# Gate logits and q.bk with the weights stationary on four column groups of TensorE

## The chip, the cores and the metric

The kernel runs on one core of one Trainium2 chip. The metric is device time in microseconds (us) of one execution, the median over several runs. Engines are called PE (TensorE), VectorE (DVE), ScalarE (ACT), POOL (GpSimd) and SyncE (SP, which only issues DMAs here).

## What is computed

One layer of a perceiver in float32, on x of 8 x 64 rows of 512 and a context of 8 x 1601 rows: cross attention, an attention with 16 heads and sigmoid scores, and a mixture of 8 experts with one expert for each row. Cut to what the change touches:

```python
# cross attention
qp = layernorm(x) @ Wq + bq
kp = ctx @ Wk + bk
logits = (qp @ kp.T) / sqrt(512)      # = (qp @ Wk.T @ ctx.T + qp . bk) / sqrt(512)
x = x + softmax(logits) @ (ctx @ Wv + bv)
# ... attention with 16 heads ...
# experts, on layernorm(x)
logits = xn @ gate_w.T                # 8 logits for each row
top_v, sel = max(logits), argmax(logits)
rw = sigmoid(top_v)                   # xs = xn * rw goes to expert sel
```

## The kernel before

The 512 rows of x are four tiles of 128 rows (two batches each, called a pair p, or tile i). All products are float32; a row of 512 is four chunks of 128 on the partitions (dc or ec).

**Order of the work.** PE's order is written out by hand over the whole kernel (`manual_schedule`); the other engines are ordered by a planner, save in a few stretches, and each runs its instructions in its order. PSUM has eight banks of one shape (`bank`); SBUF tiles come from pools: 12 slabs of 128 x 2048 (context groups, weights, xnT, qpT), 22 rows, 5 blocks (`blk`). A load into a slab is issued by SyncE when the slab's last reader is done.

**Start.** `normal`, `turn_x` and `project_q` make qpT, the projected queries with features on the partitions, first for tile 0, then for tiles 1 to 3. `keyed(p)` multiplies them with Wk (p_qk), `biased(p)` with bk: four products of 128 x 128 stationary qpT with one moving column give q.bk of the 128 rows in a PSUM column, and ScalarE copies it to `qb[:, p]`. `spread` (POOL) and `fill_queries` (PE transposes rt, ScalarE copies) lay the keyed queries out as R.

**Pair by pair.** For p in 0 to 3: the context (cx) is transposed by VectorE in blocks (`blocks`, `turn_group`, L233 and L240); `scores` multiplies them with R in four quarters q of 32 products each, into four banks sc; `softmax` uses qb in VectorE's nb and bias (L375, L377) and ScalarE's exponentials; `chance` (pp) turns them, `attend` (ac) sums the context in four groups g. In p = 0, `keyed` and `biased` of pairs 1 to 3 and `tables` come between softmax and the first `chance`. `tables` makes gwc, the gate weights less their mean, 128 x 4 x 8.

**Gates.** The second attention and the gates of tile i run inside the passes of later pairs (i = p - 2) for tiles 0 and 1 and in the hand-written tail for tiles 2 and 3. `face` transposes x into x3T; `gated` calls `gate`: four products of stationary x3T chunks with 8 moving columns of gwc (L682, pl), then on VectorE the row moments, the maximum (top), a one-hot (oh); ScalarE takes the sigmoid rw. `routed` finds the row's slot with products pr of oh and running sums, and POOL scatters the scaled rows to DRAM; `fetch` (SyncE) reads them back by expert, `flip` (t_xe, xeT), `up_first` and `up_last` (gu, four experts on four column groups of 32), `over` (ht) and `down` (y) apply the experts.

Of the kernel before, what the change touches and what calls it, by code (L numbers as in the profile page):

```python
# [36 lines left out]
def perceiver_kernel(ctx: ExitStack, tc: tile.TileContext, out: bass.AP, t: dict):  # L37
# [16 lines left out]
    def row(name):  # L54
        return rowp.tile([P, D], F32, tag="row", name=name)
# [4 lines left out]
    def bank(name):  # L60
        return banks.tile([P, D], F32, tag="bank", name=name)

    def bank4(name):
        return banks.tile([P, DC, P], F32, tag="bank", name=name)
# [37 lines left out]
    def load_b(name, n, c=None):  # L102
        if c is None:
            c = const.tile([P, n], F32, tag=name, name=f"c_{name}")
        tc.keep_in_program_order(
            nc.gpsimd.dma_start(out=c, in_=t[name].partition_broadcast(P))
        )
        return c
# [203 lines left out]
        qks[p] = row(f"qk{p}")  # L312
        nc.scalar.copy(qks[p], ps)

    def biased(p):

        cols = slice(p * P, (p + 1) * P)
        ps = bank(f"qb{p}")
        for ec in range(DC):
            nc.tensor.matmul(  # L320
                ps[:, 0:1], lhsT=qpT[:, ec, cols],
                rhs=bk[:, ec : ec + 1], start=(ec == 0), stop=(ec == DC - 1),
            )
        nc.scalar.copy(qb[:, p : p + 1], ps[:, 0:1])  # L324

    def spread(p):

# [17 lines left out]
    def fill_queries(p, R, q4s, half):  # L345
        for b0 in range(8 * half, 8 * half + 8, 4):
            tp = bank4(f"rt_{p}_{b0}")
            for j in range(4):
                nc.tensor.transpose(
                    tp[:, j, :], q4s[b0 // 4][:, j, :, :].rearrange("p a d -> p (a d)"), ident  # L350
                )
            nc.scalar.copy(R[:, b0 : b0 + 4, :], tp)
# [56 lines left out]
    def attend(p, g, pt, ac):  # L409
        cx = cxs.pop((p, g))  # L410
        nch, m = extent(g)
        for j in range(nch):
            for b2 in range(2):
                r = b2 * S
                rhs = cx[b2][:, j, :] if g < 3 else cx[b2][:m, :]
                nc.tensor.matmul(  # L416
                    ac[r : r + S, :], lhsT=pt[:m, j, r : r + S], rhs=rhs,
                    start=(g == 0 and j == 0), stop=(g == 3),
                )
# [225 lines left out]
    before = const.tile([P, P], F32, tag="before", name="before")  # L645
    iot = const.tile([P, E], I32, tag="iot", name="iot")
    rev = const.tile([P, E], F32, tag="rev", name="rev")
    gwc = const.tile([P, DC, E], F32, tag="gwc", name="gwc")

    def tables():  # L650
        nc.gpsimd.memset(ones, 1.0)
        nc.gpsimd.memset(before, 1.0)
        nc.gpsimd.affine_select(
            before, before, pattern=[[1, P]], base=0, channel_multiplier=-1,
            compare_op=ALU.is_gt, fill=0.0,
        )
        nc.gpsimd.iota(iot, pattern=[[-1, E]], base=E, channel_multiplier=0)
        nc.gpsimd.tensor_copy(rev, iot)
        ps = bank("gs")
        nc.tensor.matmul(  # L660
            ps[:, : DC * E], lhsT=ones, rhs=gwT.rearrange("p c e -> p (c e)"),
            start=True, stop=True,
        )
        mean = tiny(E, "gmean", "gmean")
        nc.vector.tensor_reduce(
            mean, ps[:, : DC * E].rearrange("p (c e) -> p e c", e=E), AX.X, ALU.add
        )
        nc.vector.tensor_scalar(mean, mean, -1.0 / D, None, ALU.mult)
        nc.vector.tensor_tensor(
            gwc, gwT, mean.unsqueeze(1).to_broadcast([P, DC, E]), ALU.add  # L670
        )

    runs = []

    def gate(i):


        x3T = tile_of[i]["x3T"]
        ps = bank(f"pl{i}")
        pl = ps[:, :E]  # L680
        for dc in range(DC):
            nc.tensor.matmul(  # L682
                pl, lhsT=x3T[:, dc, :], rhs=gwc[:, dc, :],
                start=(dc == 0), stop=(dc == DC - 1),
            )
        mean, rs = spread_v(xs[i], f"c{i}")

        top = tiny(1, "top", f"top{i}")
        nc.vector.tensor_reduce(top, pl, AX.X, ALU.max)
        nc.scalar.activation(rw[:, i : i + 1], top, AF.Sigmoid, scale=rs)  # L690
        wt = tiny(E, "wt", f"wt{i}")
        nc.vector.scalar_tensor_tensor(wt, pl, top, rev, ALU.is_equal, ALU.mult)
        first = tiny(1, "first", f"first{i}")
        nc.vector.tensor_reduce(first, wt, AX.X, ALU.max)
        nc.vector.tensor_scalar(oh[:, i, :], wt, first, None, ALU.is_equal)

        begin = tiny(1, "begin", f"begin{i}")
        skip = (NT - 2) * PART * (E - 1) if i == NT - 1 else 0
        nc.vector.tensor_scalar(begin, first, -PART, E * PART + skip, ALU.mult, ALU.add)
        return mean, rs, begin  # L700
# [114 lines left out]
    def face(i):  # L815
        x3T = row4(f"x3T{i}")
        nc.scalar.copy(x3T, transposed(xs[i], f"x3_{i}"))
        tile_of[i]["x3T"] = x3T

    def gated(i):  # L820
        d = tile_of[i]
        d["spread"] = gate(i)
# [23 lines left out]
    def do(*steps):  # L846
        for f, i in steps:
            f(i)

    with tc.manual_schedule(engines={mybir.EngineType.Activation}):  # L850
        keyed(0)
        for i in range(1, NT):
            turn_x(i, later[i - 1])
        biased(0)
    q4s = spread(0)
    project_q(1, NT - 1, [bank(f"qp1_{ec}") for ec in range(DC)])
    R = queries(0)
    fill_queries(0, R, q4s, 0)
    fill_queries(0, R, q4s, 1)
    bv = load_b("xbv", D, row("c_xbv"))  # L860
    lnw = load_late("lnw", [P, DC])
    lnb = load_late("lnb", [P, DC])
# [9 lines left out]
    for p in range(NT):  # L872
        i = p - 2
        if 0 < p < NT - 1:
            q4s = spread(p + 1)
        sc = [bank(f"sc_{p}_{a}") for a in range(4)]
        for q in range(4):
            if p == 0 and q == 0:
                nTs = [first[1, 0], first[1, 1]]
            elif p == 0 and q == 1:  # L880
                nTs = [first[2, 0], blocks(0, 2, 1)]
            else:
                nTs = quarter(p, q + 1) if q < 3 else None
            if i >= 0 and q == 3:
                scores(p, q, R, sc, Ts, range(3))
                do((back, i))
                scores(p, q, R, sc, Ts, (3,))
            else:
                scores(p, q, R, sc, Ts)
            Ts = nTs  # L890
            if i >= 0 and q < 3:
                do(((split, align, sums)[q], i))
        L, r = softmax(p, sc)
        pts = []

        def chance():
            pts.append(chances(p, len(pts), L))

        if p == 0:
            for k in range(1, NT):  # L900
                keyed(k)
                biased(k)
                if k == 1:
                    q4s = spread(1)
            tables()
        else:
            do((at_turn, p - 1))
            if i >= 0:
                do((output, i))
        if p + 1 < NT:  # L910
            R = queries(p + 1)
            if p == 0:
                chance()
                fill_queries(1, R, q4s, 0)
            elif p == 1:
                fill_queries(2, R, q4s, 0)
                do((at_out, 0))
                chance()
            else:
                do((at_out, p - 1))  # L920
                fill_queries(p + 1, R, q4s, 0)
                chance()
            fill_queries(p + 1, R, q4s, 1)
        else:
            at_out(p - 1, chance)
        if 0 < p < NT - 1:
            load_pair(p + 1)
        if p == 1:
            blank_rows()
        ac = bank(f"ac_{p}")  # L930
        if i >= 0:
            do((face, i))
        for g in range(4):
            if g < 3:
                chance()
            if p > 0 and g == 3:
                do((turn, p - 1))
            attend(p, g, pts[g], ac)
            if p > 0 and g == 0:
                do((norm, p - 1))  # L940
            if i >= 0 and g == 0:
                do((gated, i))
            if i >= 0 and g == 1:
                do((routed, i))
        tile_of[p]["acs"] = divided(p, ac, r)
        if 0 < p < NT - 1:
            do((unit_q, p - 1))
            Ts = quarter(p + 1, 0)
            do((unit_k, p - 1), (gates, p - 1), (values, p - 1))
        elif p == 0:  # L950
            Ts = quarter(1, 0)
# [82 lines left out]
    do((unit_q, 3), (over, 0), (sums, 2))  # L1034
    unit_k(3, lambda: back(2))
    do((flip, 1), (output, 2))
    do((split, 3), (gates, 3), (face, 2), (values, 3), (gated, 2), (align, 3), (up_first, 1))
    do((routed, 2))
    fetch(1)
    do((sums, 3), (up_last, 1), (back, 3), (down, 0), (output, 3), (over, 1), (flip, 2))  # L1040
    do((flip, 3), (face, 3), (up_first, 2), (gated, 3), (up_last, 2), (routed, 3))
    fetch(2)

    ps = bank("pc")
# [128 lines left out]
```

## Time and profile before

| what | us |
| --- | --- |
| median of 3 runs | 298.19 |
| lowest and highest | 298.16, 298.40 |
| the profiled execution | 297.94 |
| its span, from the first to the last instruction | 296.2 |

One execution is profiled, on the chip. "Busy" of PE is from the start of a product to its modelled end, and products overlap, so the mean of a row is a latency and the distance between starts is what a product costs. PEld is the load of stationary weights. The busy row of forty slices gives tenths of 7.4 us each. In a group, the numbers after the first bar are busy us and mean ns, those after the second the idle time of the engine just before, and what ended most of it. A timeline row has start, length, engine, line, operation and tiles (out<-in), the shape, the count, and in brackets the idle time before it with its releaser. A SyncE wait row has the total, the number and the longest.

### The profile page before, as it was taken

The numbers are of one execution on the slowest core, as the hardware profiler recorded it, in microseconds if no ns is written. First come the engines' busy times: TensorE is split into PE (matmuls) and PEld (weight loads), VectorE is DVE, ScalarE is ACT, GpSimd is POOL, SyncE is SP. The second block draws the span as 40 slices with busy tenths as digits, with TensorE's granted clock in tenths as the row PEclk, the third lists the DMA queues.
The fourth block names the chain that finished last, engine by engine and source line by source line (L and its number), as shares of the span: only waits on it lengthen the run. The fifth ranks groups of instructions, "written<-read, shape, count | busy, mean of one in ns | idle before, by whom it ended". The sixth has DMA issues, their size and how long they took to land. (4 is left out here: it accounts for less than half of the span.)

```text
span 296.2 us, 6460 instructions
## 1 busy us (share of the span) xinstructions
PE 284.2 (96%) x2652; PEld 145.4 (49%) x2652; DVE 159.0 (54%) x412; ACT 92.1 (31%) x202; POOL 64.0 (22%) x109
## 2 busy tenths in 40 slices
PE   6999899999999999999999999999999999999992
PEld 4866655653654334655634465544455456353320
DVE  2464477226654377856668795463272457364140
ACT  2222304340019121236814143651515534120110
POOL 4065200600071101600211310032050032412302
PEclk9999999999999999999999999999999999999998
DMA  6999970179986895000199300959991200523501
GB/s 186 350 408 397 340 318 1 19 284 358 424 292 226 289 385 214 6 3 0 24 387 379 135 2 10 358 198 318 383 375 67 73 0 2 173 74 113 175 3 42
DMA packets 20288, 57.71 MB, mean 195 GB/s; under 512 B 2274, under 2 KB 10514, under 8 KB 16544
## 3 DMA queue, kind: packets, MB, share of 16 engines
q1 hardware_dynamic: 17568, 50.37, 47.5%
q0 software_dynamic: 2400, 6.89, 6.2%
q8 instruction: 23, 0.38, 0.5%
q14 instruction: 9, 0.07, 0.1%
q10 hardware_dynamic: 288, 0.00, 0.1%
HBM read 50.94 MB, written 6.84 MB: 195 GB/s over the span
## 5 line engine op out<-in xcount | busy, mean ns | idle before, releaser
L233 DVE STREAM_TRANSPOSE T<-cx 128x512 f32<-128x512 f32 x96 | 61.8, 680 | 25.2 <-DMA cx<-in_ctx_dram 18.6
L360 PE MATMUL sc<-T,R 32*64 32x416 f32 (+2 forms) x1024 | 49.5, 501 | 1.8 <-DVE T L233 1.2
L416 PE MATMUL ac<-cx,pt 128*64 128x512 f32 x192 | 43.8, 598 | 0.0
L360 PEld LDWEIGHTS sc<-T,R 32*64 32x64 f32 x1024 | 26.6, 131 | 19.3 <-issue 7.1
L416 PEld LDWEIGHTS ac<-cx,pt 128*64 128x64 f32 x192 | 12.7, 136 | 22.4 <-issue 21.6
L981 PE MATMUL gu<-wgu,xeT 128*32 128x512 f32 x192 | 23.0, 597 | 0.0
L492 POOL TENSOR_TENSOR gm_k<-qn_k,c_gk 128x512 f32<-128x512 f32 x4 | 5.1, 1271 | 61.0 <-DVE qn_k L487 61.0
L284 PE MATMUL qp<-xnT,w_xWq 128*128 128x128 f32 (+1 forms) x64 | 16.3, 426 | 0.5 <-ACT xnT L275 0.5
L455 POOL TENSOR_TENSOR x<-x,c_bo 128x512 f32<-128x512 f32 x4 | 5.1, 1270 | 54.3 <-DVE xh L454 54.3
L332 POOL COPY q<-qk 128x512 f32<-128x512 f32 x16 | 9.0, 612 | 34.5 <-ACT qb L324 21.4
L185 PE MATMUL p_qk<-w_xWkT,qpT 128*128 128x512 f32 x32 | 14.9, 605 | 0.0
L185 PE MATMUL p_q<-w_aWq,xhT 128*128 128x512 f32 x32 | 14.8, 605 | 0.0
L185 PE MATMUL p_k<-w_aWk,xhT 128*128 128x512 f32 x32 | 14.7, 595 | 0.0
L185 PE MATMUL p_po<-w_xWv,acT 128*128 128x512 f32 x32 | 14.7, 595 | 0.0
L406 ACT COPY pt<-pp 128x512 f32<-128x512 f32 (+1 forms) x16 | 8.3, 516 | 20.4 <-PE pp L404 20.2
L185 PE MATMUL p_o<-w_aWo,cT 128*128 128x512 f32 x32 | 14.5, 596 | 0.0
L371 DVE TENSOR_REDUCE mx<-sc 128x1 f32<-128x416 f32 (+2 forms) x16 | 8.1, 567 | 11.9 <-PE sc L360 11.9
L185 PE MATMUL p_v<-w_aWv,xvT 128*128 128x512 f32 x32 | 14.4, 592 | 0.0
L284 PEld LDWEIGHTS qp<-xnT,w_xWq 128*128 128x128 f32 x64 | 11.6, 232 | 5.0 <-ACT xnT L275 0.9
L1016 PE MATMUL y<-wd,hT 128*32 128x512 f32 x96 | 11.5, 596 | 0.6 <-DVE hT L1008 0.6
L981 PEld LDWEIGHTS gu<-wgu,xeT 128*32 128x32 f32 x192 | 6.0, 109 | 8.9 <-issue 8.2
L185 PEld LDWEIGHTS p_q<-w_aWq,xhT 128*128 128x128 f32 x32 | 5.7, 189 | 9.0 <-issue 5.9
(190 smaller groups left out, 392.1 us busy)
## 6 DMA issues: line engine op xcount, KB each, us to landing
cx<-in_ctx_dram SPq DMA_DIRECT2D x24, 1024.0 KB, 10.0
wgu<-in_wgT_dram SPq DMA_DIRECT2D x8, 512.0 KB, 9.5
wgu<-in_wuT_dram SPq DMA_DIRECT2D x8, 512.0 KB, 10.3
wd<-in_wdT_dram SPq DMA_DIRECT2D x8, 512.0 KB, 8.9
rd<-blank POOLq DMA_DIRECT2D x6, 258.0 KB, 4.8
in<-rd SPq DMA_DIRECT2D x6, 258.0 KB, 4.6
xd<-blank POOLq DMA_DIRECT2D x6, 256.0 KB, 4.6
in<-xd SPq DMA_DIRECT2D x6, 256.0 KB, 7.2
```

The costliest lines, as they stand in the source:

```text
L185: nc.tensor.matmul(ps, lhsT=srcT[:, dc, :], rhs=w[:, dc, :], start=(dc == 0), stop=(dc == DC - 1),)
L233: nc.vector.transpose(T[:, :, 128 * g : 128 * g + 128].rearrange("p b (c k) -> p b c k", k=32), cxs[p, g][b2][:, :, 128 * q : 128 * q + 12 ...
L284: nc.tensor.matmul(ps[ec][:, : n * P], lhsT=wq[:, dc, ec * P : (ec + 1) * P], rhs=xnT[:, dc, cols], start=(dc == 0), stop=(dc == DC - 1),)
L332: nc.gpsimd.tensor_copy(q4, qk[:, 32 * b0 : 32 * b0 + 128].rearrange("p (b d) -> p b d", d=32).unsqueeze(2).to_broadcast([P, 4, 4, 32]),)
L360: nc.tensor.matmul(sc[a][r : r + S, : WIDTH[a]], lhsT=R[32 * a : 32 * a + 32, b, r : r + S], rhs=Ts[b2][32 * a : 32 * a + 32, j, : WIDTH[a ...
L371: nc.vector.tensor_reduce(mx[:, a : a + 1], sc[a][:, : WIDTH[a]], AX.X, ALU.max)
L406: nc.scalar.copy(pt[:m, :nch, :], tp[:m, :nch, :])
L416: nc.tensor.matmul(ac[r : r + S, :], lhsT=pt[:m, j, r : r + S], rhs=rhs, start=(g == 0 and j == 0), stop=(g == 3),)
L455: nc.gpsimd.tensor_tensor(xs[i], xs[i], bo, ALU.add)
L492: nc.gpsimd.tensor_tensor(heads(gm), heads(qn), gb.unsqueeze(1).to_broadcast([P, H, HD]), ALU.mult)
L981: nc.tensor.matmul(ps[c, :], lhsT=xTs[k][:, dc, c], rhs=ffw[e][0][:, dc, :], start=(dc == 0), stop=(dc == DC - 1),)
L1016: nc.tensor.matmul(y[c, :], lhsT=hT[:, ic, c], rhs=ffw[e][1][:, ic, :], start=(ic == 0), stop=(ic == IC - 1),)
```

## The change

`biased` now serves all pairs at once. The stationary operand is a chunk of bk, one column repeated 32 times; the moving operand is qpT of one pair, 128 columns. Pair p writes PSUM partitions 32p to 32p + 31, so the four pairs use the four groups of 32 columns of the array. ScalarE copies the result (qbT), `unturned` transposes it on PE after quarter 0 of the first scores, and VectorE copies every 32nd column to qb. The four calls of `biased(p)` go.

The gate is cut in two. `gate_parts` (new step `logits`) holds the gate weights stationary, padded to 32 columns (POOL fills gwc with zeros first), with x3T moving; chunk dc writes partitions 32dc to 32dc + 31, so each group holds a partial sum. ScalarE copies it to `shares`. `gate` then adds the four parts and turns them by one product of stationary shares with the 0/1 table `pick` (made from the identity by VectorE). Between the two halves stand: for tiles 0 and 1 the transposes of the next `chance`, for tile 2 the products of `align`, for tile 3 the transposes of `flip(3)`, which before came ahead of `face(3)`.

```diff
-    def biased(p):
-        cols = slice(p * P, (p + 1) * P)
-        ps = bank(f"qb{p}")
+    def biased():
+        ps = bank("qb")
         for ec in range(DC):
-            nc.tensor.matmul(
-                ps[:, 0:1], lhsT=qpT[:, ec, cols],
-                rhs=bk[:, ec : ec + 1], start=(ec == 0), stop=(ec == DC - 1),
-            )
-        nc.scalar.copy(qb[:, p : p + 1], ps[:, 0:1])
+            for p in range(NT):
+                nc.tensor.matmul(
+                    ps[32 * p : 32 * p + 32, :P],
+                    lhsT=bk[:, ec : ec + 1].to_broadcast([P, 32]),
+                    rhs=qpT[:, ec, p * P : (p + 1) * P],
+                    start=(ec == 0), stop=(ec == DC - 1),
+                )
+        qbT = rowp.tile([P, P], F32, tag="row", name="qbT")
+        nc.scalar.copy(qbT, ps[:, :P])
+        return qbT
+
+    def unturned(qbT):
+        tp = bank4("t_qb")
+        nc.tensor.transpose(tp[:, 0, :], qbT, ident)
+        nc.vector.tensor_copy(qb, tp[:, 0, ::32])
...
-    gwc = const.tile([P, DC, E], F32, tag="gwc", name="gwc")
+    gwc = const.tile([P, DC, 32], F32, tag="gwc", name="gwc")
+    pick = const.tile([P, E], F32, tag="pick", name="pick")
...
+        nc.gpsimd.memset(gwc, 0.0)
         nc.vector.tensor_tensor(
-            gwc, gwT, mean.unsqueeze(1).to_broadcast([P, DC, E]), ALU.add
+            gwc[:, :, :E], gwT, mean.unsqueeze(1).to_broadcast([P, DC, E]), ALU.add
+        )
+        nc.vector.tensor_reduce(
+            pick, ident.rearrange("p (c k) -> p k c", k=32)[:, :E, :], AX.X, ALU.add
         )
...
+    def gate_parts(i):
+        x3T = tile_of[i]["x3T"]
+        ps = bank(f"pg{i}")
+        for dc in range(DC):
+            nc.tensor.matmul(
+                ps[32 * dc : 32 * dc + 32, :P], lhsT=gwc[:, dc, :], rhs=x3T[:, dc, :],
+                start=True, stop=True,
+            )
+        shares = rowp.tile([P, P], F32, tag="row", name=f"shares{i}")
+        nc.scalar.copy(shares, ps[:, :P])
+        return shares
+
     def gate(i):
-        x3T = tile_of[i]["x3T"]
         ps = bank(f"pl{i}")
         pl = ps[:, :E]
-        for dc in range(DC):
-            nc.tensor.matmul(
-                pl, lhsT=x3T[:, dc, :], rhs=gwc[:, dc, :],
-                start=(dc == 0), stop=(dc == DC - 1),
-            )
+        nc.tensor.matmul(pl, lhsT=tile_of[i]["shares"], rhs=pick, start=True, stop=True)
...
         keyed(0)
         for i in range(1, NT):
             turn_x(i, later[i - 1])
-        biased(0)
...
     fill_queries(0, R, q4s, 1)
+    qbT = biased()
...
+            if p == 0 and q == 0:
+                unturned(qbT)
...
                 keyed(k)
-                biased(k)
...
+            if i >= 0 and g == 1:
+                do((gated, i))
             attend(p, g, pts[g], ac)
...
             if i >= 0 and g == 0:
-                do((gated, i))
+                do((logits, i))
...
-    do((split, 3), (gates, 3), (face, 2), (values, 3), (gated, 2), (align, 3), (up_first, 1))
+    do((split, 3), (gates, 3), (face, 2), (values, 3), (logits, 2), (align, 3), (gated, 2), (up_first, 1))
...
-    do((flip, 3), (face, 3), (up_first, 2), (gated, 3), (up_last, 2), (routed, 3))
+    do((face, 3), (up_first, 2), (logits, 3), (flip, 3), (gated, 3), (up_last, 2), (routed, 3))
```

More of the change, by code (lines that the diff above doesn't have):

```diff
@@ L818, in face, with logits @@
         tile_of[i]["x3T"] = x3T
+    def logits(i):
+        tile_of[i]["shares"] = gate_parts(i)
     def gated(i):
```

## Prediction, made before the result

> **What bounds the kernel now.** I read the busy table first, then the forty slices, then the groups, the timelines of the stages that the diff touches, and SyncE's own waits. The page:
>
> ```profile
> span 296.2 us, 6460 instructions
> PE 284.2 (96%) x2652; PEld 145.4 (49%) x2652; DVE 159.0 (54%) x412; ACT 92.1 (31%) x202; POOL 64.0 (22%) x109
> ...
> PE   6999899999999999999999999999999999999992
> ```
>
> TensorE (PE) is busy in nearly the whole span, from slice 7 to the last but one without a gap. Its instruction order is written by hand. What leaves PE in that stretch should leave the span; what leaves PE earlier, where slices 5 and 6 show 8 and 9, has to be looked at one wait at a time. The chain of waits names only the last scatter, so I don't lean on it. The operations that the diff replaces, in the groups kept apart by shape:
>
> ```profile
> L981 PE MATMUL gu<-wgu,xeT 128*32 128x512 f32 x192 | 23.0, 597 | 0.0
> ...
> L682 PE MATMUL pl<-gwc,x3T 128*128 128x8 f32 x32 | 4.1, 255 | 0.0
> ...
> L320 PE MATMUL qb<-c_xbk,qpT 128*128 128x1 f32 x32 | 3.8, 240 | 0.0
> ```
>
> Four gates of four products are 16 products but 32 records, so each f32 product is two passes. The column "128*32" of gu is rows times columns of the array in use. The means are latencies; spacing is what costs, and the timeline has it:
>
> ```profile
> 45.41 3.70 PE L185 MATMUL p_qk<-w_xWkT,qpT 128*128 128x512 f32 x8
> ...
> 48.95 0.95 PE L320 MATMUL qb<-c_xbk,qpT 128*128 128x1 f32 x8
> ...
> 49.76 3.68 PE L185 MATMUL p_qk<-w_xWkT,qpT 128*128 128x512 f32 x8
> ...
> 53.28 0.95 PE L320 MATMUL qb<-c_xbk,qpT 128*128 128x1 f32 x8
> ...
> 54.09 3.68 PE L185 MATMUL p_qk<-w_xWkT,qpT 128*128 128x512 f32 x8
> ```
>
> From one p_qk to the next 4.35 and 4.33 us pass; eight passes of p_qk take 3.43 (p_k to p_v: 110.03 to 113.47 = 3.44). So one `biased(k)` costs 0.90 us of PE for one useful column: eight weight loads 0.11 apart.
>
> **What the Trainium skill says.** "TensorE: Matmul & The Clock Gate", LDWEIGHTS: a load costs by its columns, about P/1.2 ns, 107 ns for 128. The trace agrees: 0.90 / 8 = 0.11 us. "TensorEngine Tiling (Array Packing)", Performance Considerations: with few moving columns, swap stationary and streaming and use column tiles; and Key Properties: changing the tiling mode drains the array. The trace shows both: gu on four column groups runs 16 passes of 512 columns in 1.92 us, the time of four, and between modes the starts are 0.08 to 0.15 us further apart (pl to the al products, ht to gu). No row of before has four column groups with only 128 moving columns.
>
> **The change part by part.** Times are from the profiled execution: 297.94 us with a span of 296.2, 0.25 under the median 298.19.
>
> 1. `biased(0)` goes from ahead of the second q projection. Worth 0: that projection starts at 18.86 because ScalarE's xnT copies end at 18.80; PE then idles for those 0.9 us. If that cover were gone it would gain 0.9.
>
> 2. `biased()` for all pairs comes after the first R transposes: 16 products, 32 passes, four groups at a time, so 8 rounds. A round is one pass of 128 columns, 0.11 us (transposes start 0.109 apart): 0.88, and a drain 0.1, about 1.0 us. It lies ahead of the scores, which wait:
>
> ```profile
> 31.12 0.91 PE L360 MATMUL sc<-T,R 32*64 32x416 f32 x2
> ...
> 33.26 8.64 PE L360 MATMUL sc<-T,R 32*64 32x416 f32 x192 [1.23 <-DVE T L233]
> ...
> 36.38 1.90 DVE L233 STREAM_TRANSPOSE T<-cx 128x512 f32<-128x512 f32 x3 [2.59 <-PE sc L360]
> ...
> 42.15 0.26 DVE L240 STREAM_TRANSPOSE T<-tail 96x128 f32<-96x128 f32 x1
> ...
> 42.47 3.02 PE L360 MATMUL sc<-T,R 32*64 32x416 f32 x62 [0.57 <-DVE T L240]
> ```
>
> Scores start at 31.12 but stand until 33.26 for VectorE's blocks, which wait for the context's DMA. 2.14 us of cover for 1.0: worth 0. ScalarE's copy qbT (0.27, as the 128x128 hT copy takes) comes after the R copies, ahead of 16 us in which ScalarE waits.
>
> 3. `unturned`: after quarter 0 of the scores PE does one transpose (0.11, two mode changes: about 0.35 in all), and VectorE copies four columns, between two block transposes. VectorE is the bound here: from 36.38 it makes three pairs of blocks without a pause and PE waits 0.57 for the last. PE's 0.35 fits into the 0.57. VectorE's first block transpose runs 36.38 to 37.0 while PE turns qbT (ready near 36.7), so no new wait; the copy inserts 0.05 (as small operations between transposes do at 153.2) to 0.2: **+0.1**. Queued behind it are the blocks of quarters 2 and 3, which PE waits for.
>
> 4. `biased(1..3)` go from between the p_qk: 3 x 0.90 = **-2.70**, on PE where it has no gap; three copies of one column (0.16) leave ScalarE. What must keep up: ScalarE's exponentials end at 52.6 in either case, then it copies qk1; POOL's q4 copies run 53.3 to 55.6, and their transposes come on PE near 56.4. ScalarE's six copies after that end near 59.5, before attend needs more than the first. The loads of pair 1 wait on SyncE for slabs:
>
> ```profile
> SPq L212 <- PE p_qk L185: 27.4, 1, 27.4
> ...
> SPq L212 <- PE qb L320: 0.4, 1, 0.4
> ```
>
> The slab of WkT comes free with the last p_qk (issue at 57.80), that of qpT with the last qb; both come 1.7 to 2.5 us earlier, on a DMA idle since 44 us. So the pair's blocks move along, and all later loads hang on PE releases.
>
> 5. Gates 0 and 1, inside attend:
>
> ```profile
> 146.41 1.06 PE L682 MATMUL pl<-gwc,x3T 128*128 128x8 f32 x8
> ...
> 147.33 0.64 PE L404 MATMUL pp<-ident,L 128*128 128x128 f32 x4
> ...
> 147.89 3.65 PE L416 MATMUL ac<-cx,pt 128*64 128x512 f32 x16
> ```
>
> Before: 1.48 us from pl to ac. After: pg 2 rounds 0.22, drain 0.1, pp 0.44, pl as one product 0.22, drain 0.12: 1.10, if shares is there. Its chain: pg's last pass is issued at +0.11 and lands +0.28 later, ScalarE follows 0.09 on, copies 0.27, PE 0.05 on: +0.80, against PE at +0.76. Nearly a tie. Bounds: 0 gained if ScalarE is 0.4 late, 0.38 at best; I take **-0.25 each**. The sigmoid's table load (1.28) now stands after the pt copy; the row weight is then ready near 149.9, VectorE needs it by 151.9 (its wait for pr). Covered.
>
> 6. Gate 2: from the end of p_v to gu 1.91 us before. After: 0.1 + 0.22 + 0.1 + 1.02 (al with its drain) + 0.22 + 0.1 = 1.76; I take **-0.1** (0 to -0.2). The row index of tile 2 now waits behind all four sigmoids, about 0.8 later: cg ends near 253.9 where PE turns it at 254.0, and its scattered rows land near 258.9 where PE needs them at 260.1. Both covered, the first barely.
>
> 7. Gate 3: pg shares the mode of gu, but moving one transpose behind it uncovers ScalarE's xeT copy and the change of modes twice: 0 (-0.1 to +0.2).
>
> 8. POOL's fill of gwc (0.2, near 4 us; POOL idles till 17.4) and VectorE's pick (0.2, near 11 us, 1.2 us ahead of a wait for ScalarE): 0. POOL now copies xb (0.6 to 0.86) ahead of run for tiles 1 and 2: run would end near 198.5 and 249.8, PE needs it at 200.8 and 250.8. The new tiles take PSUM banks and row buffers whose last readers end several us earlier: no wait counted.
>
> Sum: 0 + 0 + 0.1 - 2.70 - 0.50 - 0.1 + 0 = **-3.2**: 294.74 for that execution, 295.0 beside the median.
>
> **Rivals.**
> - *Column groups run one after another at 128 columns* (slower). Then pg is 8 x 0.11 = 0.89 instead of 0.22, four times +0.67 = +2.7; and qb is 3.55 + 0.1, 1.5 past its cover. -3.2 + 2.7 + 1.5 = +1.0: 299.2. It decides from 0.38 us a round. Against it: gu and the scores overlap in full; for it: no row with so few columns, and weights read with a stride of 0. 0.05.
> - *The shares come late.* Each gate is a round trip over ScalarE; 0.3 more in each: +1.2, 296.2. For it: a tie in step 5 and ScalarE in program order. 0.12.
> - *The loads of pair 1 don't follow.* VectorE's last block for the next scores ends at 72.78, they start at 73.84: 1.06 of slack. Were those landings fixed, 2.6 - 1.06 = 1.5 is lost: 296.5. Against it: the wait on p_qk above. 0.08.
> - *The change does nothing where it says*: true of step 1 alone, counted at 0.
>
> **How the numbers follow.** The forecast has 0.75. Its own range is 294.5 (gates 0 and 1 at -0.38, gate 2 at -0.2, gate 3 at -0.1, copy 0.05: -3.7) to 295.9 (gates 0 to 2 at nothing, gate 3 and the copy at +0.2: -2.3). The range given, 294.4 to 296.5, takes this in and the two middle rivals; left out are the slow rival and some 0.1 of misjudged sizes. About 0.2% (0.6 us) is what a measurement of this kernel can tell from no change. Faster 0.94: the forecast and the two middle rivals, less 0.01; within 0.2% that 0.01; slower 0.05.
>
> **What would show it.** p_qk 3.43 apart; qb as 32 passes within about 1.0 us, ended before the block wait; the wait of 0.57 before quarter 3 nearly gone and quarter 3 starting near 42.6; gs near 55.8 instead of 58.42; pl's two passes directly behind pp with an idle of under 0.1; scores of pair 1 near 71.3. Wrong: qb or pg passes 0.11 apart without overlap, PE idle before pl of 0.3 or more, or a PE wait for blocks near 71.

## The result, and the profile after

| what | before | after |
| --- | --- | --- |
| median, us | 298.29 (298.16 to 299.95, 4 runs) | 295.28 (294.35 to 295.65, 4 runs) |
| the profiled execution | 297.94 | 295.09 |
| its span | 296.2 | 293.4 |

The ratio is 0.9879, 95% interval 0.9839 to 0.9919: faster by 3.0 us at the median, 2.85 between the two profiled executions. The page of after, busy table and slices:

```profile
span 293.4 us, 6477 instructions
...
PE 279.1 (95%) x2661; PEld 138.3 (47%) x2661; DVE 159.6 (54%) x414; ACT 93.2 (32%) x203; POOL 63.9 (22%) x110
...
PE   5689999999999999999999999999999999999991
```

TensorE is still busy without a gap from the fourth slice to the last but one, and it has nine records more than before (2661 against 2652) in 5.1 us less of busy time. The groups of after, kept apart by shape, say why:

```profile
L695 PE MATMUL pg<-x3T,gwc 128*32 128x128 f32 x32 | 1.7, 282 | 0.0
...
L708 PE MATMUL pl<-pick,shares 128*128 128x8 f32 x8 | 1.5, 262 | 0.0
...
L320 PE MATMUL qb<-qpT,c_xbk 128*32 128x128 f32 x32 | 1.1, 276 | 0.0
```

qb has 32 records as before. Before, 32 records of 240 ns were busy for 3.8 us together, two at a time; now 32 of 276 ns are busy for 1.1 us, eight at a time: that is how four column groups look in this view. TensorE's timeline of the p_qk stretch, to gs, the product of `tables` that stands behind the last p_qk; the first row is of before, the others of after:

```profile
58.42 0.39 PE L660 MATMUL gs<-c_gwT,ones 128*128 128x32 f32 x2
...
45.84 10.57 PE L185 MATMUL p_qk<-w_xWkT,qpT 128*128 128x512 f32 x24
56.25 0.30 PE L670 MATMUL gs<-c_gwT,ones 128*128 128x32 f32 x2
```

Three blocks of p_qk are now one row of 24 passes, 10.41 us to gs where it was 13.01 (45.41 to 58.42). The slabs follow it. SyncE's waits name the product that comes behind the last p_qk:

```profile
SPq L212 <- PE gs L670: 25.7, 1, 25.7
```

The start of pair 0, timeline of TensorE and VectorE:

```profile
31.65 1.08 PE L320 MATMUL qb<-qpT,c_xbk 128*32 128x128 f32 x32
32.66 3.97 PE L369 MATMUL sc<-T,R 32*64 32x416 f32 x64
...
32.85 1.31 DVE L233 STREAM_TRANSPOSE T<-cx 128x512 f32<-128x512 f32 x2 [1.29 <-DMA cx<-in_ctx_dram]
36.57 0.33 PE L332 MATMUL t_qb<-ident,qbT 128*128 128x128 f32 x1
36.74 0.71 DVE L233 STREAM_TRANSPOSE T<-cx 128x512 f32<-128x512 f32 x1 [2.58 <-PE sc L369]
36.83 9.09 PE L369 MATMUL sc<-T,R 32*64 32x416 f32 x192
37.38 0.12 DVE L333 COPY qb<-t_qb 128x4 f32<-128x4 f32 x1
...
42.58 0.27 DVE L240 STREAM_TRANSPOSE T<-tail 96x128 f32<-96x128 f32 x1
```

qb takes 1.01 us to the first score. VectorE's second pair of blocks waits for the context's DMA until 32.85, 0.36 later than before (32.49), and the VectorE row at 36.74 is 0.36 later too (36.38): the loads were late in this execution, qb was not what held it. Scores of quarters 1 to 3 are one row of 9.09 us without a wait in brackets; before, a wait of 0.57 us cut it. Gate 0:

```profile
144.50 0.43 PE L695 MATMUL pg<-x3T,gwc 128*32 128x128 f32 x8
...
144.85 0.66 PE L413 MATMUL pp<-ident,L 128*128 128x128 f32 x4
145.05 0.27 ACT L700 COPY shares<-pg 128x128 f32<-128x128 f32 x1 [1.34 <-PE pg L695]
...
145.36 0.39 PE L708 MATMUL pl<-pick,shares 128*128 128x8 f32 x2
...
145.68 3.65 PE L425 MATMUL ac<-cx,pt 128*64 128x512 f32 x16
```

From pg to ac 1.18 us, where pl to ac was 1.48. ScalarE's copy ends at 145.32 and pl starts at 145.36, with no wait: the tie that the prediction worked out.

TensorE's waits over the whole span; of these rows, two bear on the start:

```profile
PE p_qk L185 <- DMA w_xWkT<-in_xWkT_dram: 2.9, 1, 2.9
...
PE qp L284 <- ACT xnT L275: 1.3, 2, 0.8
```

The 0.8 is the idle time in the place of `biased(0)`. The 2.9 lies ahead of all that was changed on TensorE: the first projection was done at 10.70 us, where it took until 13.02 before, and stood until its next weights had landed. p_qk of pair 0 then started at 13.56 instead of 12.86.

### The profile page after: what moved, and what is told of

The parts are those of the page before. It is cut to its first block, busy times and chain, and to the rows that moved or that the text cites. A ratio compares the mean times of both kernels' runs of the same rounds, so it can differ in the third digit from the quotient of the medians.

```text
span 293.4 us, 6477 instructions
## 1 busy us (share of the span) xinstructions
PE 279.1 (95%) x2661; PEld 138.3 (47%) x2661; DVE 159.6 (54%) x414; ACT 93.2 (32%) x203; POOL 63.9 (22%) x110
## 5 line engine op out<-in xcount | busy, mean ns | idle before, releaser
L185 PE MATMUL p_qk<-w_xWkT,qpT 128*128 128x512 f32 x32 | 14.2, 598 | 2.9 <-DMA w_xWkT<-in_xWkT_dram 2.9
L284 PE MATMUL qp<-xnT,w_xWq 128*128 128x128 f32 (+1 forms) x64 | 14.4, 384 | 1.3 <-ACT xnT L275 1.3
L284 PEld LDWEIGHTS qp<-xnT,w_xWq 128*128 128x128 f32 x64 | 9.7, 191 | 5.7 <-ACT xnT L275 1.8
L185 PEld LDWEIGHTS p_qk<-w_xWkT,qpT 128*128 128x128 f32 x32 | 5.8, 190 | 10.5 <-issue 7.4
L1020 DVE TENSOR_TENSOR h<-gu,h 128x256 f32<-128x256 f32 x6 | 2.5, 424 | 14.0 <-ACT h L1019 14.0
```

The lines of the kernel that those rows point to most:

```text
L185: nc.tensor.matmul(ps, lhsT=srcT[:, dc, :], rhs=w[:, dc, :], start=(dc == 0), stop=(dc == DC - 1),)
L284: nc.tensor.matmul(ps[ec][:, : n * P], lhsT=wq[:, dc, ec * P : (ec + 1) * P], rhs=xnT[:, dc, cols], start=(dc == 0), stop=(dc == DC - 1),)
```

## The experiments

Where the first scores start depends on when pair 0's loads land, and these differ by execution. The runs on the later chips spread (before: 297.0 to 304.1), and their intervals are half a per cent wide or more, up to one per cent. So each run was also read in its trace: every TensorE instruction was matched with the same one of before, and the difference of the starts was followed along the span. "From p_qk on" is the change of that difference from the start of p_qk of pair 1 to the last product, which leaves the loads of pair 0 out.

| run | ratio to before (interval) | start of p_qk, pair 1, us | from p_qk on, us |
| --- | --- | --- | --- |
| before | 1 | 45.41 | 0 |
| after | 0.9879 (0.9839 to 0.9919) | 45.84 | -3.34 |
| after again | 0.9854 (0.9817 to 0.9892) | 45.63 | -3.36 |
| q.bk alone | 0.9886 (0.9856 to 0.9916) | 45.31 | -2.85 |
| gates alone | 0.9972 (0.9935 to 1.0009) | 45.53 | -0.67 |
| q.bk early in its old form | 0.9968 (0.9942 to 0.9995) | 47.46 | -3.55 |
| gate on one column group | 0.9973 (0.9943 to 1.0002) | 45.12 | -0.68 |
| nothing between the halves | 0.9956 (0.9931 to 0.9981) | 45.29 | -1.30 |
| slabs held longer | 0.9885 (0.9847 to 0.9924) | 44.97 | -3.15 |
| turn of q.bk early | 0.9875 (0.9834 to 0.9917) | 45.22 | -3.39 |
| memset on VectorE | 0.9888 (0.9837 to 0.9939) | 46.00 | -2.91 |
| memset and turn | 0.9867 (0.9822 to 0.9912) | 46.28 | -3.51 |
| q.bk alone, one memset more | 0.9906 (0.9875 to 0.9937) | 45.96 | -2.57 |

**q.bk alone.** The gates as before:

```diff
-    ps[32 * dc : 32 * dc + 32, :P], lhsT=gwc[:, dc, :], rhs=x3T[:, dc, :], start=True, stop=True
+    pl, lhsT=x3T[:, dc, :], rhs=gwc[:, dc, :], start=(dc == 0), stop=(dc == DC - 1)
...
-            if i >= 0 and g == 1:
-                do((gated, i))
...
-                do((logits, i))
+                do((gated, i))
```

> The q.bk part alone; the gates are those of the kernel before. Theory (the two parts add): the twelve products that stood between the p_qk passes of pairs 1 to 3 are gone, 2.70 us by the prediction's sum (the two traces: p_qk1 to gs 13.01 us before, 10.41 us after), and nothing else moves, so about 295.6 to 295.9 us, 0.991 of before. Rival (loads follow late or the gain is given back before the gates, and the gates bring more than their own sum): 296.3 or more.

Measured: 295.46 us, ratio 0.9886, and -2.85 us from p_qk on. Its timeline:

```profile
45.31 10.57 PE L185 MATMUL p_qk<-w_xWkT,qpT 128*128 128x512 f32 x24
55.71 0.30 PE L669 MATMUL gs<-c_gwT,ones 128*128 128x32 f32 x2
```

The stretch is 10.40 us to gs, as in after. q.bk carries most of the gain. (The traced execution itself took 296.24: its end came 7.1 us behind the last product, in the other traces 5.9.)

**Gates alone.** `biased(p)` as before, four calls, one ahead of the second q projection and three between the p_qk:

```diff
-    qbT = biased()
...
-            if p == 0 and q == 0:
-                unturned(qbT)
...
+                biased(k)
```

> The gate part alone; q.bk is that of the kernel before. Theory: the four gates bring 0.30, 0.30, 0.12 and 0.09 us as the two traces show them, -0.8 together, so about 297.5 us, 0.997 of before. Rival (the prediction's own sum, 0.25 + 0.25 + 0.1 + 0): 297.7. Rival (gates bring nothing by themselves; what the traces show there comes from other shifts): 298.1 to 298.5.

Measured: 298.29 us beside 299.59 of before; the interval (0.9935 to 1.0009) takes in no change, so the time alone doesn't decide between the three. The trace does: gates 0 and 1 take 1.18 us, 0.30 less, and from p_qk on it is -0.67, less than the gates' own 0.81 because 0.3 us is lost on the way to gate 0. The two parts together, -2.85 and -0.67, make -3.52; both hold a step of 0.15 us at t_xe (220.87 us of before) that nearly every run has, so it belongs to the one trace of before. Counted once, -3.37, where after has -3.34: the parts add.

The 0.3 us was the surprise. It is lost between 104 and 126 us, ahead of any gate, in after and in this run, and not with q.bk alone. It led to the last three experiments.

**q.bk early in its old form.** Sixteen products with a full stationary and one moving column, all at the new place:

```diff
-    ps[32 * p : 32 * p + 32, :P], lhsT=bk[:, ec : ec + 1].to_broadcast([P, 32]), rhs=qpT[:, ec, p * P : (p + 1) * P]
+    ps[:, p : p + 1], lhsT=qpT[:, ec, p * P : (p + 1) * P], rhs=bk[:, ec : ec + 1]
...
-            if p == 0 and q == 0:
-                unturned(qbT)
```

> The kernel after, with q.bk at the new place ahead of the scores but in the old form: sixteen products with a 128x128 stationary and one moving column, into four columns of one bank, one ScalarE copy to qb, no turning product. Theory (the form matters there because the wait for VectorE's blocks, 2.14 us, covers only part of sixteen times 0.224 = 3.58 us): scores of pair 0 start about 1.2 us later than with the new form, time 296.3 to 296.7. Rival (the place alone gives the gain; the scores are held by later blocks anyway): within 0.2 us of after, 295.1 to 295.5.

Measured: p_qk of pair 1 starts at 47.46, 1.6 us later than in after, though R was ready 1.5 us earlier in this execution; the median is 297.89, and the interval of the ratio (0.9942 to 0.9995) lies apart from that of q.bk alone. From p_qk on the run gains as after does (-3.55): what it loses lies ahead of that mark. Timeline, and from the page the granted clock of TensorE in the forty slices:

```profile
30.09 3.92 PE L320 MATMUL qb<-c_xbk,qpT 128*128 128x1 f32 x32
...
31.91 1.31 DVE L233 STREAM_TRANSPOSE T<-cx 128x512 f32<-128x512 f32 x2 [1.18 <-DMA cx<-in_ctx_dram]
33.94 12.54 PE L360 MATMUL sc<-T,R 32*64 32x416 f32 x233
38.43 1.90 DVE L233 STREAM_TRANSPOSE T<-cx 128x512 f32<-128x512 f32 x3 [5.21 <-PE sc L360]
...
PEclk9999799999999999999999999999999999999998
```

The row at 38.43 is the reason that a late first score isn't made up: VectorE waits 5.21 us, not 2.58, for the scores of quarter 0 to give its block buffers back, and the blocks of quarters 2 and 3 shift with it. From the second pair of blocks to this row it is 3.89 us in before (32.49 to 36.38), in after (32.85 to 36.74) and in the second trace of after (32.64 to 36.53); here it is 6.52 (31.91 to 38.43), 2.6 more.

Not all of this is the length of the old form. The 7 in the last row is a stretch from 33.3 to 36.7 us in which the granted clock was 0.5, on the first scores; no other trace has a slice below 9 ahead of its last one. Matched one by one with those of before, the scores fall back by 1.67 us inside this stretch, which leaves about 0.9 us, an estimate, for the form itself (1.2 was expected). The runs point the same way: the mean granted clock that is listed with each run is 0.993 or less in 21 of the 22 runs of this kernel and in 2 of the 10 of after, and the one run at 0.997 took 295.44 us, as long as after. So the old form does lose at this place, but in this trace more by the lower clock that came with it than by its own length. Why the clock fell isn't shown.

**Gate on one column group.** The same eight passes, one behind the other in 32 columns; ScalarE copies 32 rows, and `pick` goes:

```diff
-    ps[32 * dc : 32 * dc + 32, :P], lhsT=gwc[:, dc, :], rhs=x3T[:, dc, :], start=True, stop=True
+    ps[:32, :P], lhsT=gwc[:, dc, :], rhs=x3T[:, dc, :], start=(dc == 0), stop=(dc == DC - 1)
...
-    nc.tensor.matmul(pl, lhsT=tile_of[i]["shares"], rhs=pick, start=True, stop=True)
+    nc.tensor.matmul(pl, lhsT=tile_of[i]["shares"][:32], rhs=ident[:32, :E], start=True, stop=True)
```

> The kernel after, with the four chunks' gate products added up in one column group of 32 (one after the other, eight passes) instead of four groups side by side; the product that follows takes 32 rows and the unit columns instead of the 0/1 sum. Theory (the side-by-side groups carry the gain): eight passes in series at 0.11 us are 0.89 us against 0.43 us from first to last in after, about +0.45 to +0.65 us per gate, so +1.8 to +2.6 us, 297.1 to 297.9. Rival (the gain is from taking sixteen products with a full stationary away, whether they overlap or not): +0.3 us or less, 295.6 at most.

Measured, gate 0 on the timeline:

```profile
143.63 1.06 PE L691 MATMUL pg<-x3T,gwc 128*32 128x128 f32 x8
...
144.62 0.66 PE L413 MATMUL pp<-ident,L 128*128 128x128 f32 x4
...
145.21 0.38 PE L704 MATMUL pl<-ident,shares 32*128 32x8 f32 x2
...
145.52 2.80 PE L425 MATMUL ac<-cx,pt 128*64 128x512 f32 x12
```

From pg to ac 1.89 us: 0.71 over after and 0.41 over the old gate. The other three cost 0.71, 0.64 and 0.76 over after, 2.8 in all, and from p_qk on the run has -0.68 against -3.34. Swapping the operands without the column groups would have made each gate slower. The Trainium skill, "TensorEngine Tiling (Array Packing)", Performance Considerations, names the swap and the column tiling as one measure; here the second half of it is the whole gain.

**After again.** The kernel after, unchanged, on the chip of the three runs told next.

> The kernel after once more, on the chip of the three runs that follow, so that they can be compared with it. Theory: 0.990 of before, as the first timing had it (0.9879, 0.9839 to 0.9919), and the traces' own shift of TensorE, 2.8 us.

Measured: 0.9854, and -3.36 us from p_qk on against -3.34 in the first trace. The gain repeats, and the reading by traces repeats within 0.02 us.

**Nothing between the halves.** pl directly behind pg:

```diff
-            if i >= 0 and g == 1:
-                do((gated, i))
...
-                do((logits, i))
+                do((logits, i), (gated, i))
...
-    ... (logits, 2), (align, 3), (gated, 2), ...
+    ... (logits, 2), (gated, 2), (align, 3), ...
-    ... (logits, 3), (flip, 3), (gated, 3), ...
+    ... (logits, 3), (gated, 3), (flip, 3), ...
```

> The kernel after, with the 0/1 product of each gate directly behind its four column groups: nothing between them on TensorE. Theory (the trip through ScalarE, 0.43 us from the groups' end to the product's start, is free only because pp, al or t_xe lie over it): TensorE idles about 0.5 us at each gate, +1.9 us over after in all, and the waits name ScalarE's shares. Rival (the trip is short or absorbed later, the place doesn't matter): +0.5 us or less.

Measured: -1.30 us from p_qk on, 2.06 behind after on the same chip (-3.36). TensorE's waits show a row that after doesn't have:

```profile
PE pl L708 <- ACT shares L700: 1.7, 4, 0.4
```

Four waits, 1.7 us; gate by gate, from pg to what follows, it is 0.48, 0.48, 0.51 and 0.54 us over after. In time it is apart from after too (0.9956, 0.9931 to 0.9981, against 0.9817 to 0.9892). The placement of pp, al and t_xe between the halves is worth 2.0 us, more than the gates' whole gain of 0.8: without it the new gates would have cost time.

**Slabs held longer.** One product more, unused, that reads qpT and wkT behind the transposes of pair 1:

```diff
             fill_queries(p + 1, R, q4s, 1)
+            if p == 0:
+                last_read = bank("held")
+                nc.tensor.matmul(
+                    last_read[:, :1], lhsT=qpT[:, 0, :P], rhs=wkT[:, 0, 0:1], start=True, stop=True
+                )
```

> The kernel after, with one product more (one column, unused) that reads qpT and wkT behind the work that followed p_qk of pairs 1 to 3, so that the buffers that these hold come free about 2.2 us later, as in the kernel before. Theory (the gain of the p_qk stretch reaches the end only because the loads of pair 1 start earlier with it, and their slack is about 1.1 us): scores of pair 1 start 1.2 us later than in after, time +1.0 to +1.5 us. Rival (the loads are early enough in any case): +0.2 us, the product's own time.

Measured: a miss for the theory; the rival, the product's own time, fits (-3.15 against -3.36 of after again). SyncE's first issue for pair 1 came at 58.04, 2.67 us behind gs instead of 0.19, yet scores of pair 1 started 15.52 us behind gs instead of 15.34. VectorE's timeline of this run:

```profile
62.87 1.30 DVE L233 STREAM_TRANSPOSE T<-cx 128x512 f32<-128x512 f32 x2 [5.99 <-DMA cx<-in_ctx_dram]
65.36 3.09 DVE L233 STREAM_TRANSPOSE T<-cx 128x512 f32<-128x512 f32 x5 [1.19 <-DMA cx<-in_ctx_dram]
68.37 0.27 DVE L240 STREAM_TRANSPOSE T<-tail 96x128 f32<-96x128 f32 x1
69.03 1.30 DVE L233 STREAM_TRANSPOSE T<-cx 128x512 f32<-128x512 f32 x2 [0.40 <-DMA cx<-in_ctx_dram]
```

In after the five blocks and the tail come last, from 67.25 to 70.53. Here the planner put the two blocks of the latest load behind them, so that VectorE ends at 70.34, 14.97 us behind gs and not 14.28. A delay of 2.5 us became one of 0.7, and the slack of 1.06 took that. That the loads follow is true, and against a delay of this size it wasn't needed.

**Turn of q.bk early.** t_qb and VectorE's copy ahead of the first scores:

```diff
+    unturned(qbT)
     Ts = [first[0, 0], first[0, 1]]
...
-            if p == 0 and q == 0:
-                unturned(qbT)
```

> The kernel after, with the turning product of q.bk and VectorE's copy ahead of the first scores, in the wait for the blocks, instead of behind them. Theory (the copy on VectorE stands in the chain of blocks, 0.12 us, and that chain sets when quarter 3 starts): quarter 3 starts 0.1 us earlier against the landing of the blocks, time -0.1 us, hardly to be told from after. Rival (the trip over ScalarE holds the first scores): +0.3 us or more.

Measured: VectorE's chain, from its first block after quarter 0 to the last tail, takes 6.03 us (36.19 to 42.22), as before the change (36.38 to 42.41), where after takes 6.10 (36.74 to 42.84). 0.07 us, too little for the times to show (0.9875 against 0.9854 of after).

**Memset on VectorE.** The lost 0.3 us has two parts in the traces. Up to 110 us TensorE waits for VectorE's xhT (rows of the second attention, transposed) behind the landings of pair 2: it loses 0.18 in after, 0.39 in this run, between nothing and 0.24 in the others; that is loads. The second is nearly the same in each run that has it: from t_q, the transposes ahead of the second attention's scores, to al, their products, TensorE takes 3.87 us in before and with q.bk alone, and 4.05 in after. The timeline of after shows where it comes from:

```profile
114.53 0.69 DVE L496 TENSOR_TENSOR qn_k<-p_k,ss_k 128x512 f32<-128x512 f32 x1
115.74 1.29 POOL L501 TENSOR_TENSOR gm_k<-qn_k,c_gk 128x512 f32<-128x512 f32 x1 [19.88 <-DVE qn_k L496]
```

qn_k, the scaled keys, ends at 115.22 and POOL's product gm_k starts 0.52 later; with q.bk alone it is 0.15. gm_k leads to al through VectorE, which does gate_k, vg and kT in this order. Nothing in POOL's work there was edited; POOL only has one instruction more, far ahead: the memset of gwc.

```diff
-        nc.gpsimd.memset(gwc, 0.0)
+        nc.vector.memset(gwc, 0.0)
```

> The kernel after, with the memset of gwc on VectorE instead of GpSimd, so that GpSimd's stream has as many instructions as in the kernel before. In every kernel with that memset on GpSimd the product gm_k started 0.48 us after the end of its wait (115.02 to 115.50 us), in the kernel before and in the run with q.bk alone 0.11 us, and TensorE's al came 0.2 us later for it. Theory (the one instruction more on GpSimd is what makes gm_k late): 0.11 us again, al comes without that loss, time 0.2 us below after. Rival (it comes from the gates' or q.bk's other edits): 0.48 us again, time as after.

Measured, timeline:

```profile
114.89 0.69 DVE L496 TENSOR_TENSOR qn_k<-p_k,ss_k 128x512 f32<-128x512 f32 x1
115.72 1.30 POOL L501 TENSOR_TENSOR gm_k<-qn_k,c_gk 128x512 f32<-128x512 f32 x1 [19.70 <-DVE qn_k L496]
```

From qn_k's end to gm_k 0.14 us again, and 3.86 from t_q to al. The total hides it: this execution lost 0.39 us to loads at 110 and 0.3 to a DMA wait of t_xe at 221, so it has -2.91 from p_qk on, and its ratio (0.9888) can't be told from after's.

**Memset and turn together.**

```diff
-        nc.gpsimd.memset(gwc, 0.0)
+        nc.vector.memset(gwc, 0.0)
...
+    unturned(qbT)
     Ts = [first[0, 0], first[0, 1]]
```

> The run before this one, and besides it the turning product of q.bk ahead of the first scores. Theory: the two add: 0.2 us for the memset and 0.1 us for the turn, so 0.3 us below after, 294.6 us where after takes 294.9. Rival (one of them is jitter of the loads at the start): less than 0.15 us below after.

Measured: 295.02 us, ratio 0.9867; -3.51 from p_qk on against -3.34 and -3.36 of after, and 3.87 from t_q to al. In its trace the version is ahead of after by about 0.2 us; in time that is inside the interval, so a better version isn't shown.

**q.bk alone, one memset more.** On POOL, where after has its memset, of a tile that nothing reads:

```diff
+    unread = const.tile([P, DC, 32], F32, tag="unread", name="unread")
...
+        nc.gpsimd.memset(unread, 0.0)
```

> q.bk's new form alone with the gates of the kernel before, as in the first of these runs, and one memset more on GpSimd, of a tile that nothing reads, where the kernel after has its memset. Theory (the count of GpSimd's instructions makes gm_k late): gm_k starts 0.48 us after its wait and al 0.2 us later than in the run with q.bk alone, time +0.2 us. Rival (the gates' edits make it late): gm_k 0.11 us after its wait, no change.

Measured, timeline:

```profile
114.55 0.69 DVE L496 TENSOR_TENSOR qn_k<-p_k,ss_k 128x512 f32<-128x512 f32 x1
115.76 1.30 POOL L501 TENSOR_TENSOR gm_k<-qn_k,c_gk 128x512 f32<-128x512 f32 x1 [19.78 <-DVE qn_k L496]
```

0.52 us between them again, 4.05 from t_q to al, and -2.57 from p_qk on against -2.85 without the memset. The delay comes and goes with one instruction on POOL, in both directions, and all thirteen traces agree: 0.14 or 0.15 us in the four without such a memset on POOL, 0.52 or 0.53 in the nine with one, each time at the first of the four gm_k alone (0.15 to 0.18 at the others). Why POOL needs 0.37 us more at that instruction isn't shown; the trace has no row for it.

## Why the prediction was right, point by point

The forecast was 295.0 us from a sum of -3.2; the median came to 295.28, -3.0. Its steps:

1. **`biased(0)`, worth 0: right.** In after TensorE waits 0.8 us for ScalarE's xnT in its place; with the gates alone, where `biased(0)` stays, there is no such wait between 15 and 25 us.
2. **`biased()` ahead of the scores, about 1.0 us, covered: right.** 1.01 us to the first score; VectorE's blocks moved by what their loads moved, 0.36. The same work in the old form, 3.9 us, was not covered, and came with a lower clock.
3. **`unturned`, +0.1: right**, 0.07. Quarter 3 started at 42.90, not 42.6; the 0.36 us of late landing are more than the difference.
4. **`biased(1..3)`, -2.70: right.** -2.60 up to gs, and a further 0.09 by the scores of pair 1, at 71.59 (71.3 was foreseen, before the landing's 0.36). The reason given for it, that the loads of pair 1 follow, was correct as a fact; the run with the slabs held longer shows that it wasn't a condition.
5. **Gates 0 and 1, -0.25 each: right in kind, short by 0.05.** -0.30 each. The tie between ScalarE's shares and TensorE came out to 0.04 us.
6. **Gate 2, -0.1: right.** -0.12 from the start of p_v to gu (5.34 to 5.22).
7. **Gate 3, 0 within -0.1 to +0.2:** right; -0.09, from the first t_xe to pr (6.10 to 6.01), near the good end.
8. **POOL's memset, 0: wrong by about 0.2.** Its own run time was covered as argued; what it did to a POOL instruction some 110 us later was not thought of. Neither step nor range had a term for an engine whose count of instructions matters.

Measured steps: 0.07 - 2.69 - 0.60 - 0.12 - 0.09 + 0.18 = -3.25; with the 0.36 of late loads in that execution -2.89, where the span shrank by 2.85. Three shifts that belong to no step are left out and nearly cancel: 0.18 at xhT, -0.15 at t_xe and -0.07 at pair 1's first pp. The gain of the gates stayed whole; step 8 took a quarter of it back elsewhere. That the sum came out within 0.05 of the -3.2 is in part luck: the gates gave 0.81 where 0.60 was counted, and the 0.18 of step 8, which was counted at nothing, took most of the difference back.

**The rivals.** *Column groups in series*: excluded by the 1.01 us of 32 qb passes, and priced by the run on one group, +2.8 against the +2.7 worked out. *The shares come late*: no wait on shares in after; the run with nothing between the halves shows the same trip uncovered, 0.5 us a gate. *The loads of pair 1 don't follow*: its price of 1.5 us was too high. It held VectorE's order fixed, and the planner doesn't. *Does nothing where it says*: true of step 1 alone, as counted. The 0.6 us that a measurement was said to tell from no change is too fine for these runs: their intervals reach 0.25 to 0.5% (0.7 to 1.5 us) to either side, so parts smaller than that are read from the traces alone.

## What to carry to other kernels

A pass with one or eight moving columns took 0.11 us here, as long as one with 128: swap the operands, and spread the now narrow stationaries over the column groups, because the swap alone was slower than what it replaced (1.89 against 1.48 us a gate). Put something that TensorE has to do anyway between the two halves of a trip over another engine, and take it as part of the price: here it decided between a gain of 0.8 us and a loss. Where loads at the start jitter by more than the effect, follow the difference of starts along two traces from a mark behind the jitter, and then look at each place where it steps, the unedited ones first. Look at the granted clock of the stretch as well, before a slower stretch is put down to the instructions in it.

## What the runs showed that was not expected

- One more memset on POOL, at 3.9 us and itself covered, delayed a POOL instruction at 115.7 us by 0.37 us (0.15 to 0.52 from its operand's end), 0.18 of it on TensorE. It went with the memset off POOL and came with an unused one in a kernel that had none.
- On four column groups 32 float32 passes of 128 columns took 1.01 us to the next product, 0.03 each, with a stationary operand read as one column repeated 32 times: no price for that access was seen.
- The planner turned a 2.5 us later load into a 0.7 us later end of VectorE's work by an order of its own: an edit of one engine's timing may change another's order, so a price that holds the order fixed can be wrong, as it was here (1.5 us foreseen, none measured).
- Sixteen products with one moving column kept TensorE busy from 30.09 to 34.01 us without a pause, and from 33.3 us on the granted clock was 0.5 for 3.4 us; 21 of the 22 runs of that kernel have a mean clock of 0.993 or less, against 2 of the 10 of after. The cause isn't shown.
